# Two graph layers on one core: layer 1's weights in other space, diagonals on VectorE, one GpSimd operation per norm, some stores from ScalarE's queue

## The chip, the core and the metric

The kernel runs on one core of a Trainium2 chip. A core has five engines that run side by side and wait for one another by semaphores: TensorE (PE in the profile; PEld is its weight load), VectorE (DVE), ScalarE (ACT), GpSimd (POOL) and SyncE (SP), which here only issues transfers. Transfers are issued from a queue of SP, ScalarE or GpSimd and land later. The metric is device time in microseconds, the median of three runs, lower is better.

## The reference

There are 2708 nodes with 256 features (`x`) and a dense matrix `adj` of edge weights, mostly zeros. Layer 0 mixes two propagations in two steps: `R @ x`, a walk over the row-normalised `adj` plus the identity, and `A @ x`, attention whose rows are cut to the smallest set of entries that holds 0.9 of the mass. Each is followed by a small projection; the sum is normalised, scaled by `ln_g`, shifted by `ln_b`, added to `x` and normalised again. Layer 1 is a graph attention with four heads:

```python
Wh = jnp.einsum('nd,hdo->nho', x, W)
e = jax.nn.leaky_relu(s_i[:, None, :] + s_j[None, :, :], NEG_SLOPE)
adj_sl = adj.at[idx, idx].set(1.0)
e_masked = jnp.where((adj_sl != 0)[:, :, None], e, -jnp.inf)
attention = jax.nn.softmax(e_masked, axis=1)
h_prime = jnp.einsum('ijh,jho->iho', attention, Wh)
```

Its result is added to `x` and normalised once more. `s_i` and `s_j` are the products of `Wh` with the two halves of `a`.

## The kernel before

The nodes are cut into 22 tiles, 16 of 128 rows and 6 of 110.

**Layer 0** (`fast_layer0`, L525 to L1158) makes two steps over the 22 tiles of rows. In each, one tile's attention is summed on TensorE (`weigh`, L258) while the threshold search of later tiles runs on ScalarE, VectorE and GpSimd, and pieces of the walk (`walks`, L893) fill TensorE between. `slot` (L990) is one turn: every search goes on by a piece, every finishing tile goes on by a piece, then some matmuls of the walk follow. A piece is what stands between two `yield` lines. In step 1 a finished tile passes through `finish` (L961), `norms` (L170) and `sources` (L144). `norms` normalises twice: statistics on VectorE (`bn_stats`, `bn_aggr`), then on GpSimd the addition of eps (`ve`) and the power -0.5 (`rs`), then the normalisation on VectorE. `sources` transposes and projects the tile on TensorE and stores its values, already weighted, to DRAM (`vd`, L168, SP's queue). For the last four tiles (`LATE`) these two parts are left to layer 1.

A check by VectorE, `verdict` (L1107), adds up facts of the search; a flag that it leaves in `bad` is read at the end and starts a slower general path, which these inputs don't take.

**Layer 1** (`layer1`, L1166) goes over the target nodes in three blocks of 8, 8 and 6 tiles (`spans`), called block 0, 1 and 2 here, and in each over the 22 tiles of source nodes: 66 steps in all. In block 0 the sources come in the order of `first`: tiles 8 to 17, 0 to 7, 18 to 21. A step needs:

- a mask: `neighbours` (L1186) loads a part of `adj` from SP's queue into a ring of three tiles (`adjp`), ScalarE takes Sign (L1193) and Square (L1198), so that an edge is 1. Where the source tile lies in the block itself (8, 8 and 6 steps), GpSimd sets the diagonal to 1 between the two (L1196, L1197), with `offdiag` and `ident`;
- four sets of weights, one per head: one VectorE product each (`weights`, L1272) of a maximum with the mask, into `pt` tiles, two sets deep;
- the values `v`, loaded from DRAM in block 0 (L1260), and the targets' factors, broadcast from DRAM by `spread` (L217): two tiles `e` for blocks 0 and 2, `r` for block 1;
- 16 matmuls into `acc` for the values (L1283), 16 for the denominators (L1293).

In turn n the code emits, in this order, the mask of step n+2, a piece of each late tile, a piece of each settling tile, the weights of step n+1, and the matmuls of step n. The late tiles join one per turn (L1314). At turn 11 of a block the next block's targets are shared and spread. After a block, its tiles settle one after another during the next block (`settle`, L1201): three transposes, a division on ScalarE, the addition of `xe` on GpSimd, a norm, the store (L1240). Block 2's tiles settle in a loop after the last step, with the division on VectorE. `verdict` runs in one piece in turn 17 of block 1.

**Order.** Both layers' parts stand in regions in which TensorE, ScalarE, VectorE and GpSimd each issue their instructions in the order in which the code emits them. SP's order is left to a planner, which also decides where instructions of the two regions fall among each other.

**Space.** Pools of tiles are stacked in SBUF in the order in which they are opened. Layer 1's pools `pp`, `rp`, `pj` and `keep1` take the bytes of layer 0's, which are closed by then: `heldp`, `finp`, `rowp`, `w0`, `keep` (with `xm`, which the second walk reads, `ba`, which the second attention reads, `rinv`, `qT` and `kT1`), `sortp`, `tpp`, `wk`. All tiles of a pool that lands on closed pools wait for every user of those pools.

Of the kernel before, what the change touches and what calls it, by code (L numbers as in the profile page):

```python
# [16 lines left out]
P = 128  # L17
# [27 lines left out]
def kernel(  # L45
# [60 lines left out]
    make_identity(nc, ident)  # L106
    offdiag = const.tile([P, P], F32, name="offdiag")
    nc.vector.tensor_scalar(offdiag, ident, -1.0, 1.0, op0=ALU.mult, op1=ALU.add)
    minus_half = const.tile([P, 1], F32, name="minus_half")
# [20 lines left out]
    def layernorm(dst, src, m):  # L130

        st = small.tile([P, 6], F32, name="ln_st")
        nc.vector.bn_stats(st[:m], src)
        mv = small.tile([P, 2], F32, name="ln_mv")
        nc.vector.bn_aggr(mv[:m], st[:m])
        ve = small.tile([P, 1], F32, name="ln_ve")
        nc.gpsimd.tensor_scalar(ve[:m], mv[:m, 1:2], LN_EPS, None, op0=ALU.add)
        rs = small.tile([P, 1], F32, name="ln_rs")
        nc.gpsimd.tensor_tensor(rs[:m], ve[:m], minus_half[:m], op=ALU.pow)
        nc.vector.tensor_scalar(  # L140
            dst, src, mv[:m, 0:1], rs[:m], op0=ALU.subtract, op1=ALU.mult
        )

    def sources(t, pool, room):  # L144

# [17 lines left out]
        for h in range(H):  # L163
# [3 lines left out]
            )  # L167
        nc.sync.dma_start(vd[t][:m], vt[:m])  # L168

    def norms(t, xt):  # L170

        m = rows[t]
        hh = xe[:m, t, 0:D]
        for last in range(2):
            st = small.tile([P, 6], F32, name="ln_st")[:m]
            mv = small.tile([P, 2], F32, name="ln_mv")[:m]
            nc.vector.bn_stats(st, hh)
            nc.vector.bn_aggr(mv, st)
            yield
            ve = small.tile([P, 1], F32, name="ln_ve")[:m]  # L180
            rs = small.tile([P, 1], F32, name="ln_rs")[:m]
            nc.gpsimd.tensor_scalar(ve, mv[:, 1:2], LN_EPS, None, op0=ALU.add)
            nc.gpsimd.tensor_tensor(rs, ve, minus_half[:m], op=ALU.pow)
            yield
            nc.vector.tensor_scalar(
                hh, hh, mv[:, 0:1], rs, op0=ALU.subtract, op1=ALU.mult
            )
            yield
            if not last:
                nc.gpsimd.tensor_mul(hh, hh, g_sb[:m])  # L190
                nc.gpsimd.tensor_add(hh, hh, b_sb[:m])
                nc.gpsimd.tensor_add(hh, hh, xt[:m])
                yield

# [72 lines left out]
    def general_layer0():  # L267
        with ExitStack() as l0:
# [199 lines left out]
            def finish(t, xf2, xa2):  # L468
# [22 lines left out]
                nc.vector.tensor_add(hh[:m], zp[:m, :D], xt)  # L491
                layernorm(hh[:m], hh[:m], m)
# [3 lines left out]
                layernorm(xt, hh[:m], m)  # L496

# [27 lines left out]
    def fast_layer0(ep, adjp):  # L525

        l0 = ExitStack()

        heldp, finp, rowp, w0, keep, sortp, tpp, wk = (
            l0.enter_context(tc.tile_pool(name=name, bufs=bufs))  # L530
            for name, bufs in (
                ("heldp", HELD), ("finp", 2), ("rowp", 2), ("w0", 1), ("keep", 1),
                ("sortp", 1), ("tpp", 3), ("wk", 1),
            )
# [55 lines left out]

        ba = keep.tile([P, NT, D], F32, name="ba")
        rinv = keep.tile([P, NT], F32, name="rinv")
        qT = keep.tile([P, N], F32, name="qT")
# [7 lines left out]

        kT = [wk.tile([P, HN], F32, name="junk"), keep.tile([P, HN], F32, name="kT1")]


# [356 lines left out]
        def finish(t, ac, ca, cb):  # L961

            m = rows[t]
            xt = xe[:m, t, 0:D]
            xw = rowp.tile([P, D], F32, name="xw")[:m]
            nc.vector.tensor_add(xw, ac[:m, :D], xm[:m, t, :])  # L966
            yield
            nc.scalar.activation(xw, xw, AF.Copy, scale=rinv[:m, t : t + 1])
            while t not in held:
                yield  # L970
            nc.gpsimd.tensor_add(xt, ca[:m], cb[:m])
            nc.gpsimd.tensor_add(xt, xt, xw)
# [133 lines left out]

        def verdict(pt):  # L1107

# [3 lines left out]
            for s, r in enumerate(sorted_):  # L1112
# [37 lines left out]
                total, good.rearrange("p s t -> p (s t)"), axis=AX.X, op=ALU.add  # L1150
            )
            nc.tensor.matmul(pt, total, ones, start=True, stop=True)
            nc.vector.tensor_scalar(
                bad, pt, -1.0, float(2 * NT * P), op0=ALU.mult, op1=ALU.add
# [11 lines left out]
    def layer1(ep, adjp, r=None, verdict=None):  # L1166
        l1 = ExitStack()

        pp, rp, pj, keep = (
            l1.enter_context(tc.tile_pool(name=name, bufs=bufs))  # L1170
            for name, bufs in (("pp", 2), ("rp", 1), ("pj", 2), ("keep1", 1))
        )
        ps_u = l1.enter_context(tc.tile_pool(name="ps_u", bufs=2, space=PSUM))
        ps_v = l1.enter_context(tc.tile_pool(name="ps_v", bufs=1, space=PSUM))
# [11 lines left out]
        def neighbours(g, j):  # L1186
# [5 lines left out]
            nc.sync.dma_start(bar, adjT[off[j] : off[j + 1], i0:i1])  # L1192
            nc.scalar.activation(bar, bar, AF.Sign)  # L1193
            if j in spans[g]:
                own = bar[:, off[j] - i0 : off[j + 1] - i0]
                nc.gpsimd.tensor_mul(own, own, offdiag[:k, :k])  # L1196
                nc.gpsimd.tensor_add(own, own, ident[:k, :k])  # L1197
            nc.scalar.activation(bar, bar, AF.Square)  # L1198
            return bar

        def settle(g, t, val, den, u, last):  # L1201
# [24 lines left out]
            yield  # L1226
            st = small.tile([P, 6], F32, name="ln_st")[:m]
            mv = small.tile([P, 2], F32, name="ln_mv")[:m]
            nc.vector.bn_stats(st, flat)
            nc.vector.bn_aggr(mv, st)  # L1230
            ve = small.tile([P, 1], F32, name="ln_ve")[:m]
            rs = small.tile([P, 1], F32, name="ln_rs")[:m]
            nc.gpsimd.tensor_scalar(ve, mv[:, 1:2], LN_EPS, None, op0=ALU.add)
            nc.gpsimd.tensor_tensor(rs, ve, minus_half[:m], op=ALU.pow)
            yield
            o = pp.tile([P, D], F32, name="o")[:m]
            nc.vector.tensor_scalar(
                o, flat, mv[:, 0:1], rs, op0=ALU.subtract, op1=ALU.mult
            )
            nc.sync.dma_start(out[off[t] : off[t + 1], :], o)  # L1240

# [58 lines left out]
        def prepared(t):  # L1300

            yield from norms(t, x_late[:, t - NT + LATE, :])
            yield from sources(t, pp, aux)


        late = [prepared(t) for t in range(NT - LATE, NT)] if verdict else []
        rest, running = [], []
        mask(0)
        mask(1)
        weights(0)  # L1310
        for n, (g, i, j) in enumerate(order):
# [35 lines left out]
            if last:  # L1347
                for c, (c0, w) in enumerate(cuts[g]):
                    copy = nc.scalar.copy if c == 0 else nc.vector.tensor_copy
                    copy(den[:, c0 : c0 + w], acc[2][c][:, :w])  # L1350
                assert not rest and not late
# [74 lines left out]
```

## Time and profile before

| | us |
|---|---|
| median of three runs (1613.76 to 1616.03) | 1614.43 |
| the profiled execution, its own time | 1616.12 |
| span in that profile | 1614.3 |
| TensorE busy in it | 1555.1 |
| VectorE, ScalarE, GpSimd busy | 1225.7, 758.0, 475.0 |
| last matmul of layer 0's attention ends | 1230.5 |
| first matmul of layer 1's block 0, 1, 2 starts | 1232.78, 1372.01, 1502.43 |
| last step of block 2 ends | 1588.7 |

The span runs from the first to the last instruction of the program; the time of the execution holds a little more around it. A row of the timeline gives start, duration, engine, line, operation, tiles written and read, and in brackets the idle time of the engine just before it with what ended it. A row of a stretch gives the busy time of each engine in it. Busy times of engines overlap: what a change is worth shows only where an engine's wait ends last.

### The profile page before, as it was taken

What the parts mean: (1) busy time and instruction counts of PE and PEld (TensorE: products, weight loads), DVE (VectorE), ACT (ScalarE), POOL (GpSimd) and SP (SyncE); (2) the same over time, 40 slices, a digit from 0 to 9 for tenths busy, and PEclk for the clock granted to TensorE, in tenths of its full rate; (3) what the DMA queues carried; (4) which work ended last, traced back from release to release, by engine and by line L of the source; (5) the groups of instructions that cost most, each with busy time, mean ns of one, the idle gap of its engine ahead of it and who ended that gap; (6) DMA issues with size and microseconds to landing.
All of it is one profiled execution on the core that took longest, in us unless ns stands there. A gap on an engine that the chain in (4) does not pass through costs nothing.

```text
span 1614.3 us, 23771 instructions
## 1 busy us (share of the span) xinstructions
PE 1555.1 (96%) x8029; PEld 1032.9 (64%) x8029; DVE 1225.7 (76%) x3669; ACT 758.0 (47%) x1324; POOL 475.0 (29%) x908
## 2 busy tenths in 40 slices
PE   6999999999998999999999999999999989998994
PEld 3477777776776888787778888777785322222342
DVE  2777677677309767877878888989885969999995
ACT  2444444444345455555555665556633334443441
POOL 1311000001023122232124554555533820162143
PEclk9999999999999999999999999999999999999997
DMA  7200000000034333333333334343244242342331
GB/s 200 77 13 17 9 9 12 10 9 13 8 92 107 98 86 96 91 76 84 78 97 96 99 104 118 102 110 94 73 115 148 78 150 84 97 139 77 86 95 30
DMA packets 172493, 128.26 MB, mean 79 GB/s; under 512 B 44342, under 2 KB 161804, under 8 KB 172362
## 3 DMA queue, kind: packets, MB, share of 16 engines
q1 hardware_dynamic: 166442, 115.87, 26.5%
q0 software_dynamic: 3648, 9.26, 1.8%
q10 hardware_dynamic: 2272, 1.52, 0.3%
q8 instruction: 65, 1.06, 0.3%
q14 instruction: 66, 0.54, 0.1%
HBM read 111.78 MB, written 13.46 MB: 78 GB/s over the span
## 4 chain that ended last, share of the span: by engine, by line
PE 83%; DVE 9%; DMA 3%; POOL 2%; ACT 1%; issue 1%; SPq 0%; ACTq 0%; POOLq 0%; DVEq 0%
PE att L258 25%; PE walk L893 24%; PE acc L1283 8%; PE lg L658 7%; PE tr L240 6%; DVE pt L1272 5%; PE acc L1293 4%; PE tr L938 2%; PE tr L952 2%; DMA blk<-in_adjT_dram 2%; PE tr L155 1%; PE lg L628 1%; PE tr L628 1%; DMA xa<-in_w1T_dram 0%; POOL blk L1197 0%
## 5 line engine op out<-in xcount | busy, mean ns | idle before, releaser
L245 ACT COPY eT<-tr 128x512 f32<-128x512 f32 (+5 forms) x264 | 141.5, 537 | 289.2 <-PE tr L240 286.4
L683 ACT ACTIVATE junk<-e,minus,rth 128x2708 bf16<-128x2708 f32 (+1 forms) x88 | 232.8, 2646 | 19.5 <-POOL rth L715 18.6
L1283 PE MATMUL acc<-pt,v 128*64 128x512 f32 (+3 forms) x1056 | 227.9, 560 | 5.9 <-DVE pt L1272 3.7
L258 PE MATMUL att<-ba,eT 128*128 128x256 f32 (+3 forms) x968 | 230.8, 379 | 0.7 <-ACT eT L245 0.7
L258 PE MATMUL att<-xm,eT 128*128 128x256 f32 (+3 forms) x968 | 230.9, 380 | 0.4 <-ACT xa L1021 0.4
L893 PE MATMUL walk<-xe,blk 128*128 128x257 f32 (+3 forms) x968 | 225.3, 384 | 5.0 <-DVE xf L907 5.0
L893 PE MATMUL walk<-xm,blk 128*128 128x256 f32 (+3 forms) x968 | 222.1, 380 | 1.2 <-DVE xw L966 1.2
L893 PEld LDWEIGHTS walk<-xe,blk 128*128 128x128 f32 (+3 forms) x968 | 178.4, 186 | 50.3 <-issue 12.2
L1272 DVE SCALAR_TENSOR_TENSOR pt<-e,tj,blk 128x1024 f32<-128x1024 f32 (+3 forms) x176 | 190.1, 1142 | 25.0 <-PE att L258 9.4
L893 PEld LDWEIGHTS walk<-xm,blk 128*128 128x128 f32 (+3 forms) x968 | 177.6, 186 | 35.4 <-issue 4.2
L258 PEld LDWEIGHTS att<-ba,eT 128*128 128x128 f32 (+3 forms) x968 | 169.5, 186 | 22.4 <-ACT eT L245 1.2
L258 PEld LDWEIGHTS att<-xm,eT 128*128 128x128 f32 (+3 forms) x968 | 169.5, 186 | 22.1 <-ACT xa L1021 0.8
L662 ACT ACTIVATE e<-lg 128x1024 f32<-128x1024 f32 (+1 forms) x132 | 121.1, 922 | 115.0 <-PE lg L658 111.4
L1283 PEld LDWEIGHTS acc<-pt,v 128*64 128x64 f32 (+1 forms) x1056 | 74.4, 138 | 146.2 <-issue 108.2
L763 DVE MAX8 cand<-e 128x8 f32<-128x170 f32 (+1 forms) x352 | 89.6, 322 | 90.7 <-ACT e L662 90.6
L240 PEld LDWEIGHTS tr<-ident,e 128*128 128x128 f32 (+3 forms) x968 | 115.2, 138 | 55.7 <-issue 21.0
L240 PE MATMUL tr<-ident,e 128*128 128x128 f32 (+3 forms) x968 | 147.0, 271 | 0.3 <-ACT xe L944 0.3
L1193 ACT ACTIVATE blk<-blk 128x1024 f32<-128x1024 f32 (+3 forms) x66 | 63.2, 957 | 161.4 <-DMA blk<-in_adjT_dram 148.4
L1293 PE MATMUL acc<-pt,sb 128*32 128x512 f32 (+3 forms) x1056 | 113.6, 548 | 0.0
L1272 DVE SCALAR_TENSOR_TENSOR pt<-r,tj,blk 128x1024 f32<-128x1024 f32 (+1 forms) x88 | 111.1, 1324 | 3.2 <-PE acc L1293 2.1
L763 DVE MAX8 cand<-scr 128x8 f32<-128x97 f32 (+1 forms) x616 | 102.0, 244 | 0.0
L907 DVE TENSOR_TENSOR xf<-walk,xe 128x257 f32<-128x257 f32 (+1 forms) x22 | 9.4, 426 | 110.8 <-PE walk L893 110.8
(215 smaller groups left out, 1987.5 us busy)
## 6 DMA issues: line engine op xcount, KB each, us to landing
blk<-in_adjT_dram SPq DMA_DIRECT2D x32, 704.0 KB
blk<-in_adjT_dram SPq DMA_DIRECT2D x32, 512.0 KB
blk<-in_adjT_dram SPq DMA_DIRECT2D x48, 330.0 KB
blk<-in_adjT_dram SPq DMA_DIRECT2D x32, 320.0 KB
blk<-in_adjT_dram SPq DMA_DIRECT2D x12, 605.0 KB
blk<-in_adjT_dram SPq DMA_DIRECT2D x12, 440.0 KB
blk<-in_adjT_dram SPq DMA_DIRECT2D x18, 283.6 KB
c<-cs POOLq DMA_DIRECT2D x32, 128.0 KB, 2.0
```

The lines of the kernel that those rows point to most:

```text
L240: nc.tensor.transpose(tr[: rows[t], q, :m], e[:m, off[t] : off[t + 1]], ident[:m, :m])
L245: copy(eT[:k, : len(grp), :m], tr[:k, : len(grp), :m])
L258: nc.tensor.matmul(acc, eT[: rows[t], q, :m], value(t), start=(t == 0), stop=(t == NT - 1),)
L658: nc.tensor.matmul(lg[:m, h, :w], qT[part, cols], kT[s][part, c0 : c0 + w], start=True, stop=True,)
L662: nc.scalar.activation(halves[:m, :, c0 : c0 + w], lg[:m, :, :w], AF.Exp, accum_out=zp[:m, n : n + 1],)
L683: nc.scalar.activation(junk[:m], e[:m], func, scale=rth, bias=minus1[:m], accum_out=acc)
L763: nc.vector.max(cand[:, n, :], src[:m, n * size : min(N, (n + 1) * size)])
L893: nc.tensor.matmul(ac[:m, :w], blk[: rows[j], j - j0, :m], cur[: rows[j], j, 0:w], start=(j == 0), stop=(j == NT - 1),)
L1193: nc.scalar.activation(bar, bar, AF.Sign)
L1272: nc.vector.scalar_tensor_tensor(pt[:k, :gw], targets[g][h // 2][:k, h % 2, :gw], tj[:k, j, h : h + 1], bar, op0=ALU.max, op1=ALU.mult,)
L1283: nc.tensor.matmul(acc[h // 2][c][q * FO : (q + 1) * FO, :w], v[j][:k, h, :], probs[n][h][:k, c0 : c0 + w], **at,)
L1293: nc.tensor.matmul(acc[2][c][h * 32 : (h + 1) * 32, :w], sb[:k, j, h : h + 1].to_broadcast([k, 32]), probs[n][h][:k, c0 : c0 + w], **at,)
```

## The change

1. Layer 0 opens `tpp` before `sortp`, and `ba` gets a pool of its own, `keepb`. `rinv` stays in `keep`, allocated later. Layer 1 opens `pp`, `pj`, `keep1`, `rp`; `pj` holds eight tiles in one copy instead of four in two. The values are allocated in the order of `first` instead of its reverse.
2. The diagonal is set by one VectorE maximum with `ident`, after Square. `offdiag` is gone.
3. All norms go through one generator, `layernorm`, with eps added on VectorE and only the power on GpSimd; it yields between the power and the normalisation. In `norms` the bias is added to `ca` earlier, in `finish`, and there are fewer yields.
4. The late tiles go two at a time, and `verdict` follows them as a generator, a piece per turn, so in block 0.
5. The late tiles' values and the outputs of blocks 0 and 1 are stored from ScalarE's queue, the latter one turn after the normalisation. In the last loop, tiles of odd number are divided on VectorE, the others on ScalarE.

```diff
-    offdiag = const.tile([P, P], F32, name="offdiag")
-    nc.vector.tensor_scalar(offdiag, ident, -1.0, 1.0, op0=ALU.mult, op1=ALU.add)
...
-        nc.gpsimd.tensor_scalar(ve[:m], mv[:m, 1:2], LN_EPS, None, op0=ALU.add)
+        nc.vector.tensor_scalar(ve[:m], mv[:m, 1:2], LN_EPS, None, op0=ALU.add)
         rs = small.tile([P, 1], F32, name="ln_rs")
         nc.gpsimd.tensor_tensor(rs[:m], ve[:m], minus_half[:m], op=ALU.pow)
+        yield
         nc.vector.tensor_scalar(
             dst, src, mv[:m, 0:1], rs[:m], op0=ALU.subtract, op1=ALU.mult
         )

-    def sources(t, pool, room):
+    def sources(t, pool, room, queue=nc.sync):
...
-        nc.sync.dma_start(vd[t][:m], vt[:m])
+        queue.dma_start(vd[t][:m], vt[:m])

     def norms(t, xt):

         m = rows[t]
         hh = xe[:m, t, 0:D]
-        for last in range(2):
...
-                nc.gpsimd.tensor_mul(hh, hh, g_sb[:m])
-                nc.gpsimd.tensor_add(hh, hh, b_sb[:m])
-                nc.gpsimd.tensor_add(hh, hh, xt[:m])
-                yield
+        yield from layernorm(hh, hh, m)
+        nc.gpsimd.tensor_mul(hh, hh, g_sb[:m])
+        nc.gpsimd.tensor_add(hh, hh, xt[:m])
+        yield
+        yield from layernorm(hh, hh, m)
+        yield
...
-        heldp, finp, rowp, w0, keep, sortp, tpp, wk = (
+        heldp, finp, rowp, w0, keep, tpp, sortp, keepb, wk = (
...
-                ("sortp", 1), ("tpp", 3), ("wk", 1),
+                ("tpp", 3), ("sortp", 1), ("keepb", 1), ("wk", 1),
...
-        ba = keep.tile([P, NT, D], F32, name="ba")
-        rinv = keep.tile([P, NT], F32, name="rinv")
+        ba = keepb.tile([P, NT, D], F32, name="ba")
...
+        rinv = keep.tile([P, NT], F32, name="rinv")
...
             nc.gpsimd.tensor_add(xt, xt, held.pop(t)[:m])
+            nc.gpsimd.tensor_add(ca[:m], ca[:m], b_sb[:m])
...
-        def verdict(pt):
+        def verdict(room):
...
                 if s:
+                    yield
                     nc.vector.tensor_tensor(wants, wants, haves, op=ALU.min)
...
+                    yield

                     nc.vector.tensor_tensor(more, most, nxt, op=ALU.is_equal)
...
+                    yield
...
+                yield
                 nc.vector.scalar_tensor_tensor(
                     ok, z, Z_LOW, ok, op0=ALU.is_gt, op1=ALU.mult
                 )
...
+            yield
+            pt = room()[0:1, 0, 0:1]
             nc.tensor.matmul(pt, total, ones, start=True, stop=True)
+            yield
...
-        pp, rp, pj, keep = (
+        pp, pj, keep, rp = (
...
-            for name, bufs in (("pp", 2), ("rp", 1), ("pj", 2), ("keep1", 1))
+            for name, bufs in (("pp", 2), ("pj", 1), ("keep1", 1), ("rp", 1))
         )
+        DEEP = 2
...
-        for t in reversed(first):
+        for t in first:
...
             nc.scalar.activation(bar, bar, AF.Sign)
+            nc.scalar.activation(bar, bar, AF.Square)
             if j in spans[g]:
                 own = bar[:, off[j] - i0 : off[j + 1] - i0]
-                nc.gpsimd.tensor_mul(own, own, offdiag[:k, :k])
-                nc.gpsimd.tensor_add(own, own, ident[:k, :k])
-            nc.scalar.activation(bar, bar, AF.Square)
+                nc.vector.tensor_tensor(own, own, ident[:k, :k], op=ALU.max)
             return bar
...
-            if last:
+            if last and t % 2:
                 nc.vector.tensor_tensor(
...
             o = pp.tile([P, D], F32, name="o")[:m]
-            nc.vector.tensor_scalar(
-                o, flat, mv[:, 0:1], rs, op0=ALU.subtract, op1=ALU.mult
-            )
-            nc.sync.dma_start(out[off[t] : off[t + 1], :], o)
+            yield from layernorm(o, flat, m)
+            if last:
+                nc.sync.dma_start(out[off[t] : off[t + 1], :], o)
+                return
+            yield
+            nc.scalar.dma_start(out[off[t] : off[t + 1], :], o)
...
-                probs[n] = [pj.tile([P, GW], F32, name=f"pt{h}") for h in range(H)]
+                probs[n] = [pj.tile([P, GW], F32, name=f"pt{h}_{n % DEEP}") for h in range(H)]
...
-            yield from sources(t, pp, aux)
+            yield from sources(t, pp, aux, nc.scalar)
...
         late = [prepared(t) for t in range(NT - LATE, NT)] if verdict else []
+        if verdict:
+            late.append(verdict(aux))
...
-            for part in late[: n + 1]:
+            for part in late[:2]:
...
-            if verdict and (g, i) == (1, 3 * NT // 4 + 1):
-                verdict(aux()[0:1, 0, 0:1])
```

More of the change, by code (lines that the diff above doesn't have):

```diff
@@ L173, in norms @@
         hh = xe[:m, t, 0:D]
-        for last in range(2):
[L175 to L178, printed above, removed]
-            yield
[L180 to L184, printed above, removed]
-            nc.vector.tensor_scalar(
-                hh, hh, mv[:, 0:1], rs, op0=ALU.subtract, op1=ALU.mult
-            )
-            yield
-            if not last:
-                nc.gpsimd.tensor_mul(hh, hh, g_sb[:m])
-                nc.gpsimd.tensor_add(hh, hh, b_sb[:m])
-                nc.gpsimd.tensor_add(hh, hh, xt[:m])
-                yield
+        yield from layernorm(hh, hh, m)
[4 more added lines that the diff above has]
+        yield
     GT = 8
@@ L491, in finish @@
                 nc.vector.tensor_add(hh[:m], zp[:m, :D], xt)
-                layernorm(hh[:m], hh[:m], m)
+                list(layernorm(hh[:m], hh[:m], m))
                 nc.vector.tensor_mul(hh[:m], hh[:m], g_sb[:m])
@@ L495, in finish @@
                 nc.vector.tensor_add(hh[:m], hh[:m], xt)
-                layernorm(xt, hh[:m], m)
+                list(layernorm(xt, hh[:m], m))
             for t in range(NT):
@@ L1226, in settle @@
             yield
[L1227 to L1234, printed above, removed]
-            yield
-            o = pp.tile([P, D], F32, name="o")[:m]
-            nc.vector.tensor_scalar(
-                o, flat, mv[:, 0:1], rs, op0=ALU.subtract, op1=ALU.mult
-            )
-            nc.sync.dma_start(out[off[t] : off[t + 1], :], o)
+            o = pp.tile([P, D], F32, name="o")[:m]
+            yield from layernorm(o, flat, m)
+            if last:
+                nc.sync.dma_start(out[off[t] : off[t + 1], :], o)
+                return
+            yield
+            nc.scalar.dma_start(out[off[t] : off[t + 1], :], o)
         if r is None:
@@ L1350, in layer1 @@
                     copy(den[:, c0 : c0 + w], acc[2][c][:, :w])
-                assert not rest and not late
+                assert not rest
                 rest = [(g, t, val, den) for t in span]
-            if verdict and (g, i) == (1, 3 * NT // 4 + 1):
-                verdict(aux()[0:1, 0, 0:1])
+        assert not late
         homes = [ps_v.tile([P, CHUNK], F32, name=f"acc{k}_{c}") for k in range(2) for c in range(2)]
```

## The prediction

> **What bounds the kernel now.** I read the page's busy times and chain first, then a table by stretches, then the order of the last third.
>
> ```profile
> PE 1555.1 (96%) x8029; PEld 1032.9 (64%) x8029; DVE 1225.7 (76%) x3669; ACT 758.0 (47%) x1324; POOL 475.0 (29%) x908
> PE 83%; DVE 9%; DMA 3%; POOL 2%; ACT 1%; issue 1%; SPq 0%; ACTq 0%; POOLq 0%; DVEq 0%
> 520.00:1205.00 685.00, 683.57 (x3369) 552.40 (x3368) 555.52 (x2070) 379.51 (x594) 260.08 (x552) 1.00 0.36 95
> 1222.00:1340.00 118.00, 110.20 (x587) 37.07 (x587) 94.61 (x93) 41.58 (x71) 59.26 (x46) 0.97 0.39 119
> 1460.00:1500.00 40.00, 35.55 (x199) 9.73 (x197) 36.08 (x55) 13.02 (x18) 6.67 (x5) 0.91 0.28 78
> ```
>
> The last three rows give, for a stretch, its length and the busy time of PE, PEld, DVE, ACT and POOL. TensorE is the bound; in layer 0 it is busy 683.57 of 685 us, so edits to layer 0's norms have nothing to win there. Layer 1 (from 1230.5) is where it stops. One step there costs TensorE 5.44 us in blocks 0 and 1 (1339.38 to 1344.82) and 3.62 in block 2. By that floor, with its own transposes and projections (6.7 in block 0's steps 4 to 11, 0.48 per settled tile), TensorE idles 16.5 us in block 0 (1230.55 to 1372.01), 6.7 in block 1 (to 1502.43) and 2.6 in block 2 (to 1588.6). The timeline places it:
>
> ```profile
> 1230.60 4.47 SPq L1260 DMA_DIRECT2D v<-v  x10
> 1230.62 5.33 DVE L1272 SCALAR_TENSOR_TENSOR pt<-e,tj,blk 128x1024 f32<-128x1024 f32 x4 [9.41 <-PE att L258]
> 1232.78 6.18 PE L1283 MATMUL acc<-pt,v 128*64 128x512 f32 x16 [2.25 <-DMA v<-v]
> 1247.39 5.68 DVE L1272 SCALAR_TENSOR_TENSOR pt<-e,tj,blk 128x1024 f32<-128x1024 f32 x4
> ...
> 1296.64 1.06 ACT L1198 ACTIVATE blk<-blk 128x1024 f32<-128x1024 f32 x1 [6.20 <-POOL blk L1197]
> 1299.01 1.14 PE L155 MATMUL aux<-wx,xT 128*110 128x264 f32 x4 [1.89 <-ACT xT L151]
> 1312.01 6.58 SPq L223 DMA_DIRECT2D r<-shared  x4
> 1478.42 0.19 PE L1152 MATMUL aux<-ones,total 128*1 128x1 f32 x2 [4.45 <-DVE total L1149]
> ```
>
> VectorE waits 9.4 us for attention to leave the space of the weights, so TensorE's first step takes 7.97 (1232.78 to 1240.75) instead of 5.44. Then four late norms at once put VectorE and GpSimd behind (steps 4 to 7), a GpSimd diagonal holds ScalarE, and the spread of block 1's targets holds SP, so that the next mask comes late (5.3 us at 1328 to 1339). In block 1 the lump of the verdict stops TensorE for 4.5, and 2.1 more in the step after.
>
> **What the skill says.** The Trainium skill's GPSIMD Engine Reference (Key points) says that GpSimd shares its SBUF interfaces with VectorE and contends with VectorE instructions that have two SBUF inputs. Agreed: four products take 4.87 us alone, 5.68 at 1247.39 beside three GpSimd operations. Perfetto Trace Analysis (Tensor Engine Instruction) calls VectorE, ScalarE and GpSimd strict FIFO. Agreed: the ScalarE row above sat 6.20 us behind one diagonal. DMA: Bandwidth & Descriptors (Issuing engines are not separate DMA queues) says that a store moved to ScalarE saves only issue time of the sequencer. The trace agrees on size: SP issues take 0.28 to 0.38 us, ScalarE's first two 0.44 and 0.45.
>
> **The change, part by part.**
>
> *Weights over walks and q.* A pool waits here for every user of the pools that it lands on (so the weights of before, over `keep` with `ba`, wait for attention). Adding the pools' sizes in order, `pj` now takes bytes 33,792 to 66,560 of layer 0's region: the end of `w0` and of `keep` (34,360 to about 73,200), now without `ba`. Last users there: the walk to 1220.7, ScalarE's scaling by `rinv` to 1222.3. So the first products run from 1222.4, done by 1227.4, the second set by 1233.5. The values v land on `keepb`, so they still wait for attention: TensorE still starts at 1232.78 and keeps the 2.25 idle. It gains 2.53 in step 0, and VectorE leads by a step.
>
> *Late tiles two at a time, one GpSimd operation per norm.* Extras on VectorE per step become 1.2 to 1.3 (two statistics, 0.53 each, plus the new addition, about 0.1 by the one-column operations in the trace) and 0.66 (two normalisations). TensorE can start a step while its later heads are made: the fourth is read 2.25 us after the first. That slack and the lead cover steps 0 to 9, so steps 4 to 7 lose nothing: 0.81 + 0.39 + 3.32 won. The projection no longer waits for a ScalarE held by GpSimd: 1.96 won. With 2.53 that is 9.0. In layer 0 two additions per tile move to VectorE and each norm takes three turns fewer, behind a full TensorE: nothing; if that cover fails, because GpSimd now waits for VectorE in the same turn, I allow 2 us.
>
> *Stores by ScalarE's queue.* Four v stores leave SP, where each held the masks behind it by up to 4.7 us; the output stores come a turn later, when `o` is done. Sixteen issues plus four at about 0.44 on a ScalarE with over 2 us free per step: nothing, except that SP is free.
>
> *Diagonals.* 44 GpSimd operations go; one VectorE maximum per diagonal tile comes, 22 in all. Price: the row of 256 columns beside it occupies 0.33; VectorE: DVE Perf Modes (The TRN2 errata) gives 58 + columns cycles at 0.96 GHz, an estimate of 0.19 for 128; I take 0.2. But it adds a wait. `mask(n + 2)` is emitted ahead of `weights(n + 1)`, so the maximum for step n+2 stands on VectorE before the products of n+1; before, that place was GpSimd's. Behind the maximum stand the late or settling tiles' pieces (ScalarE's division waits for `rden` among them) and the products, for which TensorE waits. The mask's load is issued when the products of n-1 end (ring of three). So two steps of VectorE take at least: 0.06 wake + load to Sign, 3.9 (mean of block 1's first seven diagonal tiles, 3.37 to 5.08) + Sign and Square 2.15 + 0.2 + extras + products 4.97 (a tenth of contention left of 4.87) = 11.3 + extras. TensorE needs 10.88 (11.36 with a settled tile).
>
> - Block 1: with 1.2 of settling every other step, 12.5 against 11.36, 1.1 over, four pairs 4.5, less 2.65 of slack: 1.9; carried step by step, with the late mask behind the second spread (load 6.6), 3.0. The verdict's 6.7 goes. Net -3.7.
> - Block 0: the spread now starts about 2.7 after step 11 begins (row, store, landing), issues 6.6, the mask behind it lands 7.5 later as now: 16.8; Sign and Square 19.0, maximum and a piece of the verdict 1.0, products of step 14 done at 25.0. TensorE wants step 14 at 16.3, and can bear 2.25: it stops 6.4. The verdict's pieces (0.8 in each of six steps; 4.5 us of small operations) add 1.9 after it. Idle 2.25 + 6.4 + 1.9 = 10.5 for 16.5: -6.0.
> - Block 2: 0.06 + 3.1 + 1.53 + 0.2 + 3.44 = 8.3, + 1.2 = 9.5 against 7.72; three pairs, 5.4, less 0.65 to 0.7: 4.7 for 2.6: +2.1.
>
> *Tail.* Six tiles pass at 2.27 each through VectorE and GpSimd. GpSimd's 0.23 plus handover 0.1 becomes about 0.1 on VectorE: -0.23 x 6 = -1.4; the first tile's division on ScalarE takes 0.92 for 0.43: +0.5. -0.9.
>
> Sum: -6.0 - 3.7 + 2.1 - 0.9 = -8.5. Against the profiled span of 1614.3 that gives 1605.8. That execution took 1616.12 with what lies around it, 1.7 above the median of 1614.43; the median moves by the same sum: **1606**.
>
> **Rivals.** *The maximum costs nothing* (masks arrive early, or the spread is queued behind more masks): then only 2.25 remains in block 0 and near nothing elsewhere. Bound: 14.3 + 6.7 + 2.6 + 0.9 = 24.5, 1590; with block 2 as forecast and little elsewhere, about 1595. For: loads without traffic reach Sign in 3.4. Against: block 1's masks are ready 5.6 after issue even without a diagonal. *VectorE becomes the bound and the gain is eaten*: contention of 0.3 per set of products and loads of 4.3 give, carried through the same steps, about 0: 1614. For: VectorE is at 114.3 of 120 us from 1340 to 1460. Against: GpSimd loses 44 of its operations beside it. *Slower*: the wait for the mask on VectorE alone. Each 1.0 that the load is longer adds 1.0 per pair, eleven pairs. From -8.5, the loss of 0.2% (+3.2) comes at 1.06 more, a mean load of 5.0; one of 5.1, the slowest ordinary diagonal one in block 1 (5.08), gives +4.7: 1619. Against: seven of them average 3.9.
>
> **How the numbers follow.** The forecast (1600 to 1611) 0.45; free maximum 0.25; eaten gain 0.13; slower 0.17. Within 0.2% is about what three runs of this kernel can't tell from no change. The range 1594 to 1618 reaches into the second and fourth case, leaving a tenth at either end; it covers the 2 us of layer 0. Faster 0.70, same 0.13, slower 0.17.
>
> **What would show it.** First products before attention ends, TensorE's first step 5.4; the v loads at 1230.6 still; no TensorE wait for `total`; VectorE waiting for ScalarE's Square in front of the maxima, nowhere else; TensorE's longest stop behind the spread, 6 us in block 0. Wrong if VectorE shows no waits at its maxima (then faster), if first products still wait for attention, or if mask loads average 5 us (then slower).

## The result, and the profile after

The changed kernel takes 1614.59 us, the kernel before 1614.43: a ratio of 0.9999, 95% interval 0.9991 to 1.0007. The forecast was 1606. The profiled execution of the changed kernel has a span of 1613.4 and took 1615.32. Nothing gained, then, and yet almost every part of the trace differs. The page's busy times and its chain:

```profile
PE 1557.3 (97%) x8029; PEld 1035.3 (64%) x8029; DVE 1227.8 (76%) x3753; ACT 761.7 (47%) x1336; POOL 391.9 (24%) x798
PE 80%; DVE 10%; DMA 5%; ACT 3%; issue 1%; POOL 1%; ACTq 0%; POOLq 0%; SPq 0%; DVEq 0%
```

GpSimd lost 83 us of work and VectorE gained 2, but neither is the bound. In the chain TensorE's share fell by three points, and those of transfers and ScalarE rose by two each: more of it now runs through masks (load, Sign, Square). The table of stretches of the changed kernel (length, then busy time of PE, PEld, DVE, ACT, POOL, then TensorE's granted clock):

```profile
520.00:1205.00 685.00, 680.25 (x3344) 549.85 (x3343) 554.10 (x2097) 379.38 (x600) 252.15 (x518) 1.00 0.36 94
1180.00:1190.00 10.00, 7.40 (x35) 5.68 (x34) 9.60 (x32) 1.40 (x4) 7.00 (x6) 0.93 0.19 50
1190.00:1200.00 10.00, 10.00 (x48) 7.91 (x47) 7.58 (x33) 2.85 (x11) 2.64 (x4) 0.90 0.55 131
1227.00:1345.00 118.00, 113.92 (x642) 38.19 (x644) 106.16 (x135) 45.49 (x74) 20.02 (x19) 1.00 0.44 127
1430.00:1470.00 40.00, 38.61 (x205) 11.31 (x203) 35.21 (x44) 14.57 (x25) 8.69 (x6) 1.00 0.43 116
```

Layer 0, where TensorE had been busy 683.57 of 685 us, lost 3.3 us of that, 2.6 of it between 1180 and 1190. The start of layer 1 (1227 to 1345, set against 1222 to 1340 before) is fuller, 113.92 for 110.20. The timeline of the changed kernel, at the places that were shown of before:

```profile
1187.84 0.38 PE L148 MATMUL tr<-ident,xe 110*128 110x110 f32 x2 [2.60 <-DVE xe L139]
...
1227.26 5.34 DVE L1258 SCALAR_TENSOR_TENSOR pt<-e,tj,blk 128x1024 f32<-128x1024 f32 x4 [0.96 <-ACT xw L953]
...
1235.50 2.70 SPq L1246 DMA_DIRECT2D v<-v  x6
1237.69 3.65 PE L1269 MATMUL acc<-pt,v 128*64 128x512 f32 x16 [2.26 <-DMA v<-v]
...
1304.07 0.28 PE L195 MATMUL aux<-ident,s_src 128*32 128x128 f32 x1 [0.68 <-ACT cs L164]
1309.15 5.45 SPq L208 DMA_DIRECT2D r<-shared  x4
1324.65 0.29 DVE L1191 TENSOR_TENSOR blk<-blk,ident 128x128 f32<-128x128 f32 x1 [4.37 <-ACT blk L1188]
1326.99 5.52 PE L1269 MATMUL acc<-pt,v 128*64 128x512 f32 x16 [0.89 <-DVE pt L1258]
...
1448.26 0.29 DVE L1191 TENSOR_TENSOR blk<-blk,ident 128x128 f32<-128x128 f32 x1 [3.47 <-ACT blk L1188]
```

Read downwards: a new wait of TensorE in layer 0 (L148). The first products at 1227.26, released by ScalarE's scaling in the walk, no longer by attention. The v loads at 1235.50, 4.9 later than before, and the first step 2.26 behind the end of attention, as before. ScalarE's 6.20 behind a GpSimd diagonal is gone. In its place maxima at the head of VectorE wait for Square: 13 of the 22, 16.6 us in all, the two longest 4.37 and 3.47. Nothing waits for the verdict any more. From the same timeline, with a step counted from its first values matmul to the next step's:

| stretch | before | after | change | forecast |
|---|---|---|---|---|
| layer 0, to the end of attention | 1230.53 | 1235.42 | +4.9 | 0 |
| block 0, from there to block 1's first matmul | 141.48 | 131.88 | -9.6 | -6.0 |
| block 1 | 130.42 | 129.19 | -1.2 | -3.7 |
| block 2, to its last matmul | 86.23 | 91.50 | +5.3 | +2.1 |
| tail | 25.60 | 25.44 | -0.2 | -0.9 |
| span | 1614.3 | 1613.4 | -0.8 | -8.5 |

So the gain of block 0 was there, larger than forecast, and layer 0 and block 2 took it back. That the sum comes out at nothing is chance. Two theories came of this. *Layer 0*: three turns fewer per tile bring one tile's normalisation to an unlucky place in VectorE's queue, and TensorE's transposes, one turn behind it, wait. *Layer 1*: the maximum, emitted ahead of the previous step's products, waits at VectorE's head for a mask. The rivals: in layer 0, GpSimd's new waits for VectorE (the allowance of 2 us in the prediction) or the other layout; in layer 1, eps on VectorE or ScalarE's stores.

### The profile page after: what moved, and what is told of

Read it like the earlier page. It is cut to its first block, busy times and chain, and to the rows that moved or that the text cites. A ratio compares the mean times of both kernels' runs of the same rounds, so it can differ in the third digit from the quotient of the medians.

```text
span 1613.4 us, 23708 instructions
## 1 busy us (share of the span) xinstructions
PE 1557.3 (97%) x8029; PEld 1035.3 (64%) x8029; DVE 1227.8 (76%) x3753; ACT 761.7 (47%) x1336; POOL 391.9 (24%) x798
## 3 DMA queue, kind: packets, MB, share of 16 engines
q10 hardware_dynamic: 5060, 4.07, 0.8%
## 4 chain that ended last, share of the span: by engine, by line
PE 80%; DVE 10%; DMA 5%; ACT 3%; issue 1%; POOL 1%; ACTq 0%; POOLq 0%; SPq 0%; DVEq 0%
PE att L243 25%; PE walk L878 23%; PE lg L643 7%; PE acc L1269 7%; PE tr L225 6%; DVE pt L1258 4%; DMA blk<-in_adjT_dram 4%; PE acc L1279 3%; PE tr L923 2%; PE tr L937 2%; ACT blk L1187 1%; PE tr L154 1%; ACT blk L1188 1%; PE lg L613 1%; DVE scr L814 1%
## 5 line engine op out<-in xcount | busy, mean ns | idle before, releaser
L1258 DVE SCALAR_TENSOR_TENSOR pt<-e,tj,blk 128x1024 f32<-128x1024 f32 (+3 forms) x176 | 186.6, 1123 | 6.6 <-PE acc L1279 4.3
L225 PEld LDWEIGHTS tr<-ident,e 128*128 128x128 f32 (+3 forms) x968 | 115.2, 139 | 56.7 <-issue 21.2
L225 PE MATMUL tr<-ident,e 128*128 128x128 f32 (+3 forms) x968 | 147.2, 271 | 1.0 <-ACT eT L230 0.6
L137 POOL TENSOR_TENSOR ln_rs<-ln_ve,minus_half 128x1 f32<-128x1 f32 (+1 forms) x66 | 65.2, 989 | 239.7 <-DVE ln_ve L135 193.3
L1258 DVE SCALAR_TENSOR_TENSOR pt<-r,tj,blk 128x1024 f32<-128x1024 f32 (+1 forms) x88 | 110.1, 1312 | 0.6 <-ACT blk L1188 0.6
```

Of the source, the lines that this page charges most:

```text
L225: nc.tensor.transpose(tr[: rows[t], q, :m], e[:m, off[t] : off[t + 1]], ident[:m, :m])
L1258: nc.vector.scalar_tensor_tensor(pt[:k, :gw], targets[g][h // 2][:k, h % 2, :gw], tj[:k, j, h : h + 1], bar, op0=ALU.max, op1=ALU.mult,)
```

## The experiments

Ratios below are to the kernel before, whose median beside them was 1614.3 to 1614.8.

**One turn more in layer 0.**

```diff
                 yield from norms(t, ca)
+                yield
                 yield from sources(t, rowp, lambda: ps_tr.tile([P, 4, P], F32, name="tr"))
```

> The kernel after with one more turn in layer 0 between a tile's second normalisation and its transposes (late tiles are left as they are). Theory (distance): the 4.9 us that layer 0 lost are TensorE waiting at the head of its queue for the normalisation of tile 17, which stands on VectorE behind a search operation of 3.47 us; a turn more (about 6 us) covers that. Attention then ends at 1230.5 to 1231.5 instead of 1235.4, no TensorE wait for xe in the walk's stretch, median 1610. Rival (GpSimd now waits for VectorE's eps addition in the same turn and holds back the search): those waits stay, attention still ends at 1234 to 1236, median 1614 to 1615.

Measured: 1611.84 us, ratio 0.9978 (0.9971 to 0.9985). Attention ends at 1230.05. The waits of this kernel from 520 to 1240 us, GpSimd's and TensorE's (microseconds in total, times, longest):

```profile
POOL ln_rs L137 <- DVE ln_ve L135: 64.3, 18, 9.3
...
PE acc L1270 <- DMA v<-v: 2.3, 1, 2.3
PE walk L878 <- DVE xw L951: 1.0, 2, 0.8
PE att L243 <- ACT eT L230: 0.6, 2, 0.4
```

and of the changed kernel, the same stretch:

```profile
POOL ln_rs L137 <- DVE ln_ve L135: 63.2, 18, 10.2
...
PE tr L148 <- DVE xe L139: 2.6, 1, 2.6
PE acc L1269 <- DMA v<-v: 2.3, 1, 2.3
PE walk L878 <- DVE xw L951: 1.3, 1, 1.3
PE tr L225 <- ACT eT L230: 0.6, 1, 0.6
```

GpSimd waits for VectorE as long as in the changed kernel (64.3 for 63.2), but TensorE's wait for `xe` is gone and so are the 4.9 us. GpSimd's waits are therefore not the cause. What made the transposes late stands in VectorE's rows of the changed kernel, and one of GpSimd:

```profile
1176.72 0.41 DVE L131 BATCH_NORM_STATS2 ln_st<-xe 110x6 f32<-110x256 f32 x1
...
1177.46 3.03 DVE L817 SCALAR_TENSOR_TENSOR e<-scr,fact,e 110x2708 f32<-110x2708 f32 x1
...
1177.62 3.27 POOL L137 TENSOR_TENSOR ln_rs<-ln_ve,minus_half 110x1 f32<-110x1 f32 x1 [6.70 <-DVE ln_ve L135]
...
1183.11 3.47 DVE L733 SCALAR_TENSOR_TENSOR scr<-e,hi 110x2708 f32<-110x2708 f32 x1
...
1187.28 0.41 DVE L139 TENSOR_SCALAR xe<-xe,ln_mv,ln_rs 110x256 f32<-110x256 f32 x1
```

Two passes of the search delay the normalisation (L139). Beside the first, 3.03 long, the power on GpSimd took 3.27 instead of the usual 0.55 and was ready at 1180.89. The normalisation comes 6.4 after that because the second pass, 3.47, and some ten small operations stand before it. That VectorE is strict FIFO is what the Trainium skill says (Perfetto Trace Analysis, Tensor Engine Instruction), and these rows agree. In the kernel before, the last normalisation ahead of a tile's transposes ended from 0.06 to 7.1 us before them, tile by tile, with the same one turn between the two; so that was never a safe distance, only one that happened to fit. Of the 4.9 us the wait is 2.6, an earlier one at 1076.8 (L225) 0.6, and TensorE then runs at half clock for 3.4 us (the 0.93 and 0.90 of the table), which costs up to 1.7: 4.9 together. A later run confirms the split: the kernel with GpSimd's diagonals has the same layer 0 and the same waits (2.61 and 0.62), but its clock did not fall after them. From the same attention matmul near 526 us to the end of attention it takes 707.4 us, the changed kernel 709.3, the kernel before 704.3.

The median fell by 2.8 only: in the profiled run block 0 is 2.3 longer than in the changed kernel (134.19 for 131.88), of it 1.5 in step 0 (6.95 for 5.44), which comes from the clock (last section); the other 0.8 is in step 14 (7.19 for 6.40).

**Layer 0's norms as before.**

```diff
-            nc.gpsimd.tensor_add(ca[:m], ca[:m], b_sb[:m])
+            if t >= NT - LATE:
+                nc.gpsimd.tensor_add(ca[:m], ca[:m], b_sb[:m])
             if t < NT - LATE:
                 yield
-                yield from norms(t, ca)
+                yield from norms0(t, ca)
```

`norms0` is `norms` as it was in the kernel before.

> The kernel after with layer 0's norms as before (eps on GpSimd, seven turns, b added on GpSimd inside the norm), layer 1 untouched. Both theories of layer 0 expect all of its loss back: attention ends at 1230.5, median 1609.5. If the loss came from the other layout of the pools or from where the planner puts instructions, attention still ends near 1235 and the median stays at 1614 to 1615.

Measured: 1606.84 us, 0.9954 (0.9942 to 0.9967). Attention ends at 1229.91: the layout and the planner took nothing. The other 2.7 us beyond expectation lie in layer 1, whose code is the same. In the profiled execution, which at 1604.74 was the fastest of this kernel's five, block 1 is 1.1 shorter, block 2 1.6, the tail 2.2. Why is open; the tail has two lengths (last section).

**The maximum a turn later**, directly ahead of the products that use it.

```diff
-            if j in spans[g]:
-                own = bar[:, off[j] - i0 : off[j + 1] - i0]
-                nc.vector.tensor_tensor(own, own, ident[:k, :k], op=ALU.max)
             return bar
...
                 bar = masks.pop(n)
+                if j in spans[g]:
+                    own = bar[:, off[j] - off[spans[g][0]] : off[j + 1] - off[spans[g][0]]]
+                    nc.vector.tensor_tensor(own, own, ident[:k, :k], op=ALU.max)
```

> The kernel after with VectorE's maximum for a diagonal emitted directly ahead of the products of its own step, a turn later than now; nothing else. Theory (the maximum waits at the head of VectorE, with the products of the step before behind it): TensorE's idle time in layer 1 falls in block 0 by 1 to 2, in block 1 from 5.5 to 1 or 2, in block 2 from 7.9 to 2 or 3; sum -9 to -11, median 1604. Rival (VectorE is too full: eps, statistics, verdict and the maxima themselves): only the 11.1 us of VectorE waits move elsewhere, block 2 stays above 90 us, median 1612 to 1615.

Measured: 1602.02 us, 0.9918 (0.9905 to 0.9931). Block 1 falls by 5.4 to 123.77, block 2 by 4.3 to 87.24, block 0 by 1.6, with step 0 at 7.00 for 5.44 by the clock: 3.2 at an equal start. VectorE in block 2 of the changed kernel, a pair of steps:

```profile
1553.23 0.27 DVE L1191 TENSOR_TENSOR blk<-blk,ident 110x110 f32<-110x110 f32 x1 [1.29 <-ACT blk L1188]
1553.42 0.42 DVE L131 BATCH_NORM_STATS2 ln_st<-res 128x6 f32<-128x256 f32 x1
...
1554.16 0.17 DVE L1202 RECIPROCAL rden<-aux 128x4 f32<-128x4 f32 x1
1554.25 3.71 DVE L1258 SCALAR_TENSOR_TENSOR pt<-e,tj,blk 128x660 f32<-128x660 f32 x4
1557.88 0.26 DVE L1191 TENSOR_TENSOR blk<-blk,ident 110x110 f32<-110x110 f32 x1
```

and with the maximum a turn later:

```profile
1549.41 0.40 DVE L139 TENSOR_SCALAR o<-res,ln_mv,ln_rs 128x256 f32<-128x256 f32 x1
1549.73 0.26 DVE L1256 TENSOR_TENSOR blk<-blk,ident 110x110 f32<-110x110 f32 x1
1550.10 3.36 DVE L1258 SCALAR_TENSOR_TENSOR pt<-e,tj,blk 110x660 f32<-110x660 f32 x4
1553.37 0.42 DVE L131 BATCH_NORM_STATS2 ln_st<-res 128x6 f32<-128x256 f32 x1
```

The same operation at the same price, but without idle time in front of it; and behind it no statistics, no `rden` and no products of another step. The rival falls: eps and stores are as in the changed kernel. The lengths of the steps concerned (us, worked out from the first values matmul of each; the floor is what TensorE's own matmuls take in a step):

| step | floor | before | after | maximum later | GpSimd diagonals |
|---|---|---|---|---|---|
| 10 | 5.44, + 2.9 projections in the three changed kernels | 6.62 | 8.36 | 8.59 | 14.59 |
| 14, 15, 16 | 5.44 each | 7.66, 8.52, 5.44 | 6.40, 7.30, 5.81 | 5.44, 5.44, 5.44 | 5.44, 5.44, 5.44 |
| 33, 35, 36, 37 | 5.92, 5.92, 5.44, 5.92 | 5.92, 5.92, 5.44, 5.91 | 6.64, 8.34, 7.30, 6.45 | 5.91, 5.92, 5.44, 6.04 | 5.92, 5.92, 5.44, 6.04 |
| 39, 40 | 5.44 each | 10.08, 7.57 | 5.44, 5.44 | 5.44, 5.44 | 5.44, 5.44 |
| 59, 61, 63, 64 | 4.10, 3.62, 3.62, 3.62 | 4.10, 3.86, 3.96, 3.84 | 5.81, 5.43, 4.97, 4.95 | 4.42, 4.74, 4.38, 3.97 | 4.29, 4.07, 4.03, 3.84 |

**Both edits.** The diff is the two above (one turn more, maximum later).

> Both edits: the turn before the transposes and the later maximum. If they act in different stretches the gains add: -4 and -10 from 1614.6, median 1600. If block 0 starts earlier but then waits for the same transfers, 1603.

Measured: 1597.80 us, 0.9899 (0.9885 to 0.9914). The two effects add: 2.8 + 12.6 = 15.4 of 16.8. The rest is of the size of the clock's part: step 0 takes 5.44 in this profile, 6.95 and 7.00 in those of the two single edits.

**GpSimd's diagonals in the changed kernel.**

```diff
             nc.scalar.activation(bar, bar, AF.Sign)
-            nc.scalar.activation(bar, bar, AF.Square)
             if j in spans[g]:
                 own = bar[:, off[j] - i0 : off[j + 1] - i0]
-                nc.vector.tensor_tensor(own, own, ident[:k, :k], op=ALU.max)
+                nc.gpsimd.tensor_mul(own, own, offdiag[:k, :k])
+                nc.gpsimd.tensor_add(own, own, ident[:k, :k])
+            nc.scalar.activation(bar, bar, AF.Square)
```

`offdiag` is back as well.

> The kernel after with the diagonals set by GpSimd between Sign and Square, as before; all else as after. Theory (the maximum at VectorE's head is what cost blocks 1 and 2): block 2 falls from 91.5 to 86 or 87, block 1 from 129.2 to 124 or 125, block 0 within 2 of after; layer 0 keeps its loss of 4.9; sum -8 to -11, median 1604 to 1607. Rival (eps on VectorE or ScalarE's stores cost there): blocks 1 and 2 stay within 2 us, median 1612 or more.

Measured: 1607.89 us, 0.9963 (0.9949 to 0.9976). Blocks 1 and 2 are back at 123.77 and 87.02, shorter by 5.4 and 4.5 (5.4 and 4.3 with the later maximum): a second way to take the wait away with the same outcome. Block 0 is 4.7 longer instead (within 2 was expected), and rows of GpSimd and ScalarE in this kernel say why:

```profile
1295.80 6.05 POOL L1192 TENSOR_TENSOR blk<-blk,offdiag 128x128 f32<-128x128 f32 x1 [4.30 <-ACT blk L1189]
...
1302.41 1.06 ACT L1194 ACTIVATE blk<-blk 128x1024 f32<-128x1024 f32 x1 [6.70 <-POOL blk L1193]
1303.38 0.57 ACT L152 COPY xT<-aux 128x220 f32<-128x220 f32 x2
```

ScalarE stood 6.70 us behind a GpSimd diagonal, with a late tile's projection (`xT`) queued behind it, so step 10 took 14.59. The diagonal itself was slow: its multiplication took 6.05 where 0.46 is enough alone. It lies beside the last five of seven products that VectorE makes without a break, and ended 0.3 after them. The wait of 6.20 that the prediction saw before the change is of the same kind: there the addition took 5.17, with four products beside it (4.86). That wait the diagonals' move was right to remove. The move was good, its place was not.

**The overlay alone**, on the kernel before.

```diff
-            for name, bufs in (("pp", 2), ("rp", 1), ("pj", 2), ("keep1", 1))
+            for name, bufs in (("pp", 2), ("pj", 1), ("keep1", 1), ("rp", 1))
...
-        ba = keep.tile([P, NT, D], F32, name="ba")
+        ba = keepb.tile([P, NT, D], F32, name="ba")
```

with `rinv` moved behind `kT1`, layer 0's pools, the names of `pt` and the order of `v` as in the change.

> The kernel before with the overlay alone: pools in the order of after, weights over walks and q, v in the order of first. Theory as forecast: first products run about 8 us before attention ends, step 0 falls from 7.97 to 5.4 and VectorE's lead of one step covers a part of the lumps of steps 4 to 8 (42.2 us for six steps of 5.44 and some extras); block 0 shorter by 3 to 6, median 1609 to 1612. Rival (step 0 was long only because TensorE ran at half clock after its idle time, and the lumps come from GpSimd and ScalarE, which the overlay doesn't touch): block 0 shorter by at most 1, median 1613 to 1615.

Measured: 1611.09 us, 0.9980 (0.9972 to 0.9988). Block 0, from the end of attention, is 4.5 shorter (136.94): step 0 5.44 for 7.97, steps 14 and 15 together 2.8 less, but steps 4 to 8 only 0.8 less, not the lumps as a whole, and steps 9 and 10 1.6 more. Both theories get a part: of the 2.5 in step 0, about 1.0 is the clock, which stood at half in the kernel before and not here.

**Late tiles two at a time, and the verdict in pieces**, on the kernel before (the pieces' `yield` lines as in the change).

```diff
-            for part in late[: n + 1]:
+            for part in late[:2]:
...
-            if verdict and (g, i) == (1, 3 * NT // 4 + 1):
-                verdict(aux()[0:1, 0, 0:1])
...
+        if verdict:
+            late.append(verdict(aux))
```

> The kernel before with two late tiles at a time, and the verdict cut into pieces behind them instead of one lump in block 1; norms, diagonals, stores and space as before. Theory: the lump of the verdict goes from block 1 (steps 39 and 40, 17.65 us, fall to 10.9: -6.7), block 0's steps 4 to 8 lose their four norms at once (-2 to -4), the verdict's pieces cost at most 1.9 in block 0. Median 1603 to 1607. Rival (the verdict's pieces and the longer run of late tiles only move the stops into block 0's steps 9 to 16): block 0 longer by 3 or more, median 1609 or more.

Measured: 1606.58 us, 0.9950 (0.9936 to 0.9963): of the two parts that were run alone on the kernel before, the larger gain. Block 1 falls by 6.7 to 123.70, exactly the verdict. In block 0 steps 4 to 8 lose 2.2 and steps 9 and 10 4.2, but steps 13 to 16, at the spread, take 4.9 more. So the rival is right there. Its causes are mixed: VectorE waits for additions of late tiles on GpSimd (1.43 and 1.66), for the mask behind the spread (3.42) and for a GpSimd diagonal that took 5.17 beside four products (1.44). In all block 0 is 2.1 shorter, about 1.0 of it in step 0, where the clock did not fall.

**Stores back to SP's queue**, in the changed kernel.

```diff
-            yield from sources(t, pp, aux, nc.scalar)
+            yield from sources(t, pp, aux)
...
-            nc.scalar.dma_start(out[off[t] : off[t + 1], :], o)
+            nc.sync.dma_start(out[off[t] : off[t + 1], :], o)
```

> The kernel after with the late tiles' v stores and the output stores of blocks 0 and 1 back on SP's queue (a turn later than before, as in after); all else as after. Forecast's term: ScalarE's issues cost nothing, SP's freedom brings something only in block 0, where a v store can hold a mask; block 0 longer by 0 to 3, blocks 1 and 2 within 0.5, median 1614 to 1617. Rival (the 20 issues at ScalarE's head delay Sign and Square and are a part of the stops at the maxima): blocks 1 and 2 shorter by 2 or more, median 1612 or less.

Measured: 1614.60 us, 0.9999 (0.9991 to 1.0008). No block moves by more than 0.4: this part is worth nothing, as the forecast had it; the rival is out.

**Old norms in layer 0 and the maximum later.** The diff is that of the two runs above.

> The kernel after with layer 0's norms as before and the maximum of a diagonal directly ahead of the products of its own step. The two gains of their own runs, -7.8 and -12.6 against 1614.6, add up to 1594; if a part of the first was the same stop that the later maximum removes (steps 33 to 36 were shorter by 1.2 in that run), 1595 to 1598.

Measured: 1595.69 us, 0.9881 (0.9865 to 0.9896). Compared with *both edits* the blocks are alike (block 0 130.30 for 128.60, with its first step at half clock, then 123.76 and 87.35 for 123.78 and 87.25); attention ends 1.2 earlier and the tail is 2.1 shorter.

**Eps on GpSimd for layer 1's settling tiles**, on top of that.

```diff
-    def layernorm(dst, src, m):
+    def layernorm(dst, src, m, eps=nc.vector):
...
-        nc.vector.tensor_scalar(ve[:m], mv[:m, 1:2], LN_EPS, None, op0=ALU.add)
+        eps.tensor_scalar(ve[:m], mv[:m, 1:2], LN_EPS, None, op0=ALU.add)
...
-            yield from layernorm(o, flat, m)
+            yield from layernorm(o, flat, m, nc.gpsimd)
```

> The kernel of the run e8_old_late with the eps addition of layer 1's settling tiles back on GpSimd (one turn as in after). Theory (block 2 is bound by VectorE, and what is left of its loss, 87.35 against 86.23 before, is eps on VectorE beside the maxima): block 2 falls to 86.5 to 86.9, the tail grows by 0.6 (0.1 a tile), block 1 stays at 123.8; median 1595 to 1597, no difference that five rounds can tell. Rival (what is left comes from the later stores or the turn between): block 2 stays at 87.3.

Measured: 1594.97 us, 0.9881 (0.9865 to 0.9896). Block 2 falls by 1.6 to 85.75 and the tail grows by 0.8, in the profiled run; the medians can't be told apart. What was left of block 2's loss was eps on VectorE. This and the kernel before it are about 1.2% faster than both kernels that were compared.

## Why the prediction was wrong

The forecast was 7.7 too low in the profiled span (-8.5 for -0.8). Two steps of it failed: that edits in layer 0 cost nothing behind a full TensorE, and the sizes of the maximum's waits in blocks 1 and 2, whose mechanism it had right. By its own steps:

- **"Behind a full TensorE: nothing", layer 0.** This step failed and is the largest error, +4.9. A full engine hides work on other engines, but it has no slack: whatever stands at its head and comes late costs its whole length. The allowance of 2 us was for GpSimd waiting for VectorE; that wait is there (63.2 us in all) and cost little: with a turn more, where it stays, attention takes 705.0 us from the matmul near 526 us, for 704.3 before. The sum treated "three turns fewer" as a pure saving, where it moves every later piece to another place in VectorE's queue.
- **Block 0, -6.0; it gave -9.6.** Start and lead came as forecast (first products 8.2 before the end of attention, for 8.1; idle 2.26 before step 0; steps 5 to 8 at 5.44). The stop behind the spread was put at 6.4 and measured 3.2, since SP put the spread behind one mask more, that of step 15 (it started 4.9 after step 11 began, not 2.7, and took 5.45, not 6.6), so that the late mask was that of step 16. The verdict's pieces, 1.9, cost nothing to be seen. And the idle time of before was summed wrong: 141.46 less 22 steps of 5.44 and 6.7 of TensorE's own is 15.1, not 16.5. With 15.1 the forecast of this block would have been -4.6; from 15.1 to the 5.5 that were left it is -9.6. And 1.0 of the 7.97 of step 0 before was clock, not weights: in the run of the late pairs, with weights in their old space and full clock, step 0 takes 6.99 (and step 1 5.84).
- **Block 1, -3.7; it gave -1.2.** The mechanism was right: the verdict's 6.7 went, the maximum put in 5.4. The stops at the maxima were sized 3.0 idle in all; they are 5.5. The term mis-sized is the mask behind the second spread. Its load to Sign was 6.80 (6.6 forecast), but it was also issued 1.88 late, SP being busy with the spread, and VectorE waited 3.47 with a whole set of products behind it. The mean load of the first seven diagonal tiles, 3.76, was right (3.9).
- **Block 2, +2.1; it gave +5.3.** Same mechanism, three terms too small. The six diagonal loads took 3.68 on average, not 3.1: 1.7 in three pairs. The trace of before could have told, with 3.62 on average; 3.11 is its shortest. The maximum takes 0.26 to 0.29, not 0.2: 0.4. And eps on VectorE was left out of the extras: 1.0 to 1.6. The price of the maximum was read from the wrong line: the Trainium skill (VectorE: DVE Perf Modes, The TRN2 errata) says below its table that the measured fixed term is about 150 cycles, not 58, and gives columns + 151 cycles at 0.96 GHz for an addition of two fp32 tensors, checked there at 512 and 2048 columns; for 128 columns that is an estimate of 0.29, and 0.28 to 0.29 were measured.
- **Tail, -0.9; it gave -0.2.** Six tiles pass 2.15 apart for 2.30, a gain of 0.15 and not 0.23, because from the end of the aggregate to the power it still takes 0.27, for 0.40 before; the first tile costs 0.5 more, as forecast.
- **Stores: nothing.** Right.

The rivals: "the maximum costs nothing" was priced at 1595, and 1595.69 is what the kernel reaches in which it waits for nothing and layer 0 loses nothing; with layer 0's loss it is 1602.02. "The gain is eaten" had 1614 right for a wrong reason: contention fell, the 88 products with `r` took 1312 ns each for 1324, and what ate the gain was a late normalisation and late masks. The slower case needed a mean load of 5.0; it was 3.76 in block 1's first seven.

## What to carry to other kernels

Emit an operation that waits for a transfer directly ahead of its first user on the same engine, not a turn early: in an in-order queue an early place is a wait for everybody behind it (12.6 us here, for 22 operations of 0.27). Where an engine is full, don't book an edit ahead of it at nothing; look at the slack of each instance at its head, and note that a shorter chain moves all of them. When a large change measures as no change, lay the stretches side by side before explaining: here +4.9, -9.6, -1.2 and +5.3 hid in -0.8.

## What the runs showed of the hardware

A short idle time can halve TensorE's clock. Step 0 follows 2.2 to 2.3 us of idle time in every profile. In five of twelve its clock then reads 0.5 for some 3 us, and with the overlay step 0 takes 6.95 to 7.13 where it takes 5.44 otherwise. The first step of the changed kernel is shown in the section on the result; the third number from the end of a stretch's row is the granted clock:

```profile
1237.69:1239.69 2.00, 2.00 (x10) 0.88 (x12) 2.00 (x2) 0.61 (x1) 1.03 (x1) 1.00 0.82 234
```

and the kernel with a turn more:

```profile
1232.33 5.16 PE L1270 MATMUL acc<-pt,v 128*64 128x512 f32 x16 [2.28 <-DMA v<-v]
1232.33:1234.33 2.00, 2.00 (x6) 0.83 (x8) 2.00 (x2) 0.46 (x1) 1.01 (x1) 0.50 0.78 248
```

It looks like a coin, but the record of the clock in the traces says more. The clock changes only at the ends of intervals of 3.413 us, a grid that runs through a whole trace (in the changed kernel it rises at 519.62 and falls at 1188.63, 196 intervals apart). Laid over TensorE's idle time from 700 to 1570 us in all twelve traces, it gives this: every interval at full clock with 1.95 us or more of idle time, eleven of them, is followed by half clock, and none with up to 1.81 is; of four at 1.89 to 1.90, three are. So a gap of 2.2 us halves the clock when it falls into one interval and not when the grid cuts it. The limit is read from few cases, and matmul ends are modelled.

The Trainium skill (TensorE: Matmul & The Clock Gate, HAM oscillation — how this bites in real kernels) warns of idle gaps of more than about 3.4 us; here 2.2 to 2.3 is enough at times. A fall in step 0 costs 1.5 to 1.7 us. It is a part of the spread of single executions: of the changed kernel's twelve, the four with a mean granted clock of 0.993 have spans of 1610.1 to 1611.8, the four at 0.990 and 0.991 spans of 1613.6 to 1615.0.

The tail has two lengths as well. GpSimd's closing drain starts 17.9 to 18.1 us after the last step in the kernels before and after, and 15.7 after it in the run with old norms; three profiles have a tail of 23.1 to 23.2 (a fourth 24.0, with the eps additions in it), the other eight 25.3 to 25.7. Nearly all of the difference lies between GpSimd's branch on `bad` and its next instruction: 0.43 us in four profiles, those three and the fourth, and 2.49 to 2.74 in the other eight. What decides isn't shown.
